# A four-layer network on one core: how attention blocks, the MLP's result and the edge layer's start leave PSUM

## The chip, the cores and the metric

The kernel runs on one core of one Trainium2 chip. The metric is the device time of one execution in microseconds (us); lower is better. Before the change it is 3922.71 us, the median of three runs from 3920.85 to 3927.91 us.

## The reference, cut to what matters

Four layers run one after the other on four images of 56 x 56 tokens with 128 channels, all in fp32. The change lies in layer 0 and at the start of layer 1.

```python
# layer 0: x = x + L0(group_norm(x))
xf = windowed_attention(shifted 7x7 windows of x) @ wo + bo      # 64 windows of 49 tokens
xf = xf + mha(layernorm(xf), wq, bq, wk, bk, wv, bv, wo, bo)     # 4 heads of 32, all 3136 tokens
h  = gelu(layernorm(xf) @ w1 + b1)                               # 128 -> 512
xf = xf + (h @ w2 + b2)                                          # 512 -> 128
# layer 1: x = x + L1(group_norm(x)), on rows of 56 nodes
edge = relu(x @ W1 [i] + x @ W2 [j] + be)                        # every pair i, j of a row
node = relu([x, edge.sum(over j)] @ Wn + bn)
```

Layers 2 (a Fourier layer with attention) and 3 (a convolution) follow. They take the second part of the span and are not touched.

## The kernel before, in words

**Layout.** Channels lie on the 128 partitions and tokens along the free dimension. An image is `xf`, 128 x 3136 fp32. A block is `NB` = 448 tokens, so an image has `NBLK` = 7 blocks. The four images go one after the other through `first_layers`: windowed attention, attention over all tokens (`fast_attention`), the MLP (`mlp`) and the edge layer (`edge_layer`). The image's input stays in `xw`, which the MLP adds back as the residual.

**Who sets the order.** In `fast_attention` and `mlp` TensorE's order is the order in which the program is written (`manual_schedule`); a scheduler places the instructions of the other engines. In the main loop of `edge_layer` the order of TensorE, ScalarE and VectorE is all as written. [...]

**Attention over all tokens.** For each block `j` of queries, 24 chunks of 128 keys and one of 64 are processed, with four heads each. TensorE writes scores into one of two PSUM tiles, `f_s0` with four banks and `f_s1` with three; ScalarE turns a whole tile into exponentials in a ring of 28 slots in SBUF (`f_ring`, line 641); TensorE multiplies these with the values into `f_po` (line 600); VectorE adds up 22 of the chunks (`f_acc`, line 594) for the denominators. At a block's end ScalarE copies `f_po` to `f_raw`, and `finish(j)` uses the next score tile: TensorE sums the exponentials over keys into its first bank (lines 607 and 610), VectorE takes the reciprocal straight out of that bank (line 612) and multiplies (line 613) into `oT`. The next scores that want this tile wait until the reciprocal has read it. `finish` is put off by some tiles (`late`, `flush`), so the next block's scores start ahead of it. After all seven blocks a loop projects each with `wo` into `f_pf`, in a pool slot that holds one bank, and VectorE adds that, with the bias, to `xf` (lines 663 and 664).

**MLP.** The tokens are taken in eight parts of 392. TensorE centres each part (`m_pc`, line 670), ScalarE squares it, TensorE averages (`n_pv`), ScalarE takes the root (line 682), and VectorE the reciprocal and the product (lines 683 and 868). Then for each part come four matmuls with GELU, and four that sum into `m_po`, of which there are two buffers. VectorE writes `xf` + `m_po` + `b2` (line 877), which frees the buffer. GpSimd adds `xw` and puts the result into image order in `x1` with three additions, since the windows are shifted by three and wrap around (lines 883 to 886). VectorE takes statistics of every seven rows (line 887).

**Start of the edge layer.** `group_norm_factors` aggregates the statistics and needs one square root on ScalarE (line 2338), after GELU was the last function there. Then VectorE normalizes all seven blocks into `e_xg` (line 192), and `project` makes `e_pa` and `e_pc` (lines 922 and 924) for the first two blocks. ScalarE copies them to `e_c` and `e_a` (lines 932 and 934). VectorE takes 9 of every 14 groups of pairs (`e_td`, line 967, straight from `e_pa` in PSUM), GpSimd and ScalarE the other 5 (`e_tp`, lines 969 and 971).

Of the kernel before, what the change touches and what calls it, by code (L numbers as in the profile page):

```python
# [11 lines left out]
F32 = mybir.dt.float32  # L12
AF = mybir.ActivationFunctionType
ALU = mybir.AluOpType
# [4 lines left out]
P = 128  # L19
# [20 lines left out]
def blk(j):  # L40
    return slice(j * NB, (j + 1) * NB)
# [149 lines left out]
def apply_norm(k, out, xt, mr):  # L191
    k.nc.vector.tensor_scalar(out, xt, mr[:, 0:1], mr[:, 1:2], ALU.subtract, ALU.mult)
# [367 lines left out]
def fast_attention(k, w, xw, xf, mr):  # L560

    nc, tc = k.nc, k.tc
    scale = 1.0 / math.sqrt(32.0)
    heads = [slice(32 * h, 32 * h + 32) for h in range(4)]
    half = (slice(0, 64), slice(64, 128))
    with ExitStack() as es:  # L570
        big = es.enter_context(tc.tile_pool(name="f_big", bufs=1))
        qT = big.tile([P, TOK], F32, name="f_qT")
        kT = big.tile([P, TOK], F32, name="f_kT")
        va = big.tile([P, 25, P], F32, name="f_va")
        fast_windows(k, w, xw, xf, mr, qT, kT, va)

        ring = es.enter_context(tc.tile_pool(name="f_ring", bufs=1)).tile([P, RING, NB], F32, name="f_ring")
        wk = es.enter_context(tc.tile_pool(name="f_wk", bufs=2))
        ps = es.enter_context(tc.tile_pool(name="f_ps", bufs=1, space=PSUM))
        oT = es.enter_context(tc.tile_pool(name="f_out", bufs=1)).tile([P, TOK], F32, name="f_oT")  # L580
        late = []
        n = 0

        def bank(turn):
            return ps.tile([P, (4, 3)[turn], 512], F32, tag="s%d" % turn, name="f_s%d" % turn)

        def slots(j, c):
            s = (96 * j + 4 * c) % RING
            return ring[:, s:s + 4, :]

        def sums(j, c, acc):

            if 0 < c < SUMMED:
                nc.vector.tensor_add(acc, slots(j, 0) if c == 1 else acc, slots(j, c))  # L594

        def values(j, c, po, p24):
            for h in range(4):
                o = half[h % 2] if c == 24 else slice(0, P)
                p = p24[o, h // 2, :] if c == 24 else slots(j, c)[:, h, :]
                nc.tensor.matmul(po[heads[h], :NB], va[o, c, heads[h]], p, start=(c == 0), stop=(c == 24))  # L600

        def finish(j, raw, acc, p24, pd):

            for c in range(SUMMED - 1, 24):
                p = acc if c < SUMMED else slots(j, c)
                for h in range(4):
                    nc.tensor.matmul(pd[heads[h], 0, :NB], k.ones[:, 0:32], p[:, h, :], start=(c < SUMMED), stop=False)
            for h in range(4):
                o = half[h % 2]
                nc.tensor.matmul(pd[heads[h], 0, :NB], k.ones[o, 0:32], p24[o, h // 2, :], start=False, stop=True)  # L610
            den = wk.tile([P, NB], F32, name="f_den")
            nc.vector.reciprocal(den, pd[:, 0, :NB])  # L612
            nc.vector.tensor_mul(oT[:, blk(j)], raw, den)

        def flush(all_=False):

            nonlocal n
            if n % 2 and not all_:
                return
            while late and (all_ or late[0][0] < n):  # L620
                _, f, *a = late.pop(0)
                if f is finish:
                    a.append(bank(n % 2))
                    n += 1
                f(*a)

        with tc.manual_schedule(engines={mybir.EngineType.PE}):
            for j in range(NBLK):
                po = ps.tile([P, 512], F32, tag="po", name="f_po")
                raw = wk.tile([P, NB], F32, name="f_raw")  # L630
                acc = wk.tile([P, 4, NB], F32, name="f_acc")
                t, done = 0, 0
                while t < 96:
                    turn, slot = n % 2, (96 * j + t) % RING
                    m = min((4, 3)[turn], RING - slot, 96 - t)
                    ss = bank(turn)
                    for i in range(m):
                        c, h = divmod(t + i, 4)
                        nc.tensor.matmul(ss[:, i, :NB], kT[heads[h], c * P:(c + 1) * P], qT[heads[h], blk(j)],  # L639
                                         start=True, stop=True)  # L640
                    nc.scalar.activation(ring[:, slot:slot + m, :], ss[:, :m, :NB], AF.Exp, scale=scale)  # L641
                    t += m
                    while 4 * (done + 1) <= t:
                        sums(j, done, acc)
                        late.append((n + 2, values, j, done, po, None))
                        done += 1
                    n += 1
                    flush()
                ss = bank(n % 2)
                for h in range(4):  # L650
                    nc.tensor.matmul(ss[half[h % 2], h // 2, :NB], kT[heads[h], 24 * P:TOK], qT[heads[h], blk(j)],
                                     start=True, stop=True)
                p24 = wk.tile([P, 2, NB], F32, name="f_p24")
                nc.scalar.activation(p24, ss[:, 0:2, :NB], AF.Exp, scale=scale)
                late.append((n + 2, values, j, 24, po, p24))
                late.append((n + 2, nc.scalar.copy, raw, po[:, :NB]))
                late.append((n + 3, finish, j, raw, acc, p24))
                n += 1
                flush()
            flush(True)  # L660
        for j in range(NBLK):
            pm = ps.tile([P, 512], F32, tag="po", name="f_pf")
            nc.tensor.matmul(pm[:, :NB], w.wo, oT[:, blk(j)], start=True, stop=True)
            nc.vector.scalar_tensor_tensor(xf[:, blk(j)], pm[:, :NB], w.fbvo, xf[:, blk(j)], ALU.add, ALU.add)


def centre(k, pool, centred, src, squares, j):
# [171 lines left out]
def mlp(k, w, xf, xw, x1, st):  # L839
# [4 lines left out]
    with ExitStack() as es:  # L844
# [25 lines left out]
        for wi, ts in enumerate(parts):  # L870
            hT = ahead
            if wi < 7:
                ahead = hidden(parts[wi + 1])
            po = psum.tile([P, 512], F32, tag="acc", name="m_po")
            for f in range(4):
                nc.tensor.matmul(po[:, :N], w.w2[:, f, :], hT[:, f, :], start=(f == 0), stop=(f == 3))
            nc.vector.scalar_tensor_tensor(xf[:, ts], po[:, :N], w.b2, xf[:, ts], ALU.add, ALU.add)
            a = xf[:, ts].rearrange("p (w i j) -> p w i j", w=8, i=7)
            x = xw[:, ts].rearrange("p (w i j) -> p w i j", w=8, i=7)
            for i0, i1 in (((0, 7),) if wi < 7 else ((0, 4), (4, 7))):  # L880
                r0 = (7 * wi + 3 + i0) % HH
                rows = x1[:, r0:r0 + i1 - i0, :]
                nc.gpsimd.tensor_add(  # L883
                    rows[:, :, 3:52].rearrange("p i (w j) -> p w i j", w=7), a[:, 0:7, i0:i1, :], x[:, 0:7, i0:i1, :])
                nc.gpsimd.tensor_add(rows[:, :, 52:56], a[:, 7, i0:i1, 0:4], x[:, 7, i0:i1, 0:4])
                nc.gpsimd.tensor_add(rows[:, :, 0:3], a[:, 7, i0:i1, 4:7], x[:, 7, i0:i1, 4:7])
                nc.vector.bn_stats(st[:, wi + (i0 > 0), :], rows.rearrange("p l n -> p (l n)"))

# [3 lines left out]
def edge_layer(k, w, x1, st):  # L894
# [9 lines left out]
    with ExitStack() as es:  # L904
# [6 lines left out]

        mr = group_norm_factors(k, wk, bank, st)
        xg = big.tile([P, TOK], F32, name="e_xg")
        for j in range(NBLK):
            apply_norm(k, xg[:, blk(j)], xf[:, blk(j)], mr)
        ready = {}

        def project(j):
            if j >= NBLK:
                return  # L920
            pa = psum.tile([P, 512], F32, tag="pa", name="e_pa")
            nc.tensor.matmul(pa[:, :NB], w.W1, xg[:, blk(j)], start=True, stop=True)
            pc = psum.tile([P, 512], F32, tag="mm", name="e_pc")
            nc.tensor.matmul(pc[:, :NB], w.W2, xg[:, blk(j)], start=True, stop=True)
            ready[j] = pa, pc

        def evacuate(j):
# [21 lines left out]
            nc.vector.scalar_tensor_tensor(xf[:, blk(j)], po[:, :NB], w.nbn, xf[:, blk(j)], ALU.max, ALU.add)  # L949

        with tc.manual_schedule(engines={mybir.EngineType.PE, mybir.EngineType.Activation, mybir.EngineType.DVE}):
            for j in range(2):
                project(j)
                evacuate(j)
            last = None
            for j in range(NBLK):
# [4 lines left out]
                for g, e in enumerate(EDGE_TURNS):  # L961
# [18 lines left out]
                        evacuate(j + 1)  # L980
                    if g == 7 and last:
                        finish(last[0], po)
                    if g == 9:
                        nc.vector.tensor_reduce(rest, c[:, :, 0:nd], AX.X, ALU.add)
                sums = wk.tile([P, 4, NB], F32, name="e_sums")
# [1480 lines left out]
```

## Time and profile before

| Image 0, us from the start of the span | what | TensorE clock granted | TensorE busy |
|---|---|---|---|
| 157 to 526 | attention over all tokens, seven blocks | 1.00 | 353.56 of 369 |
| 526 to 544 | last reciprocal, and the projections with `wo` | 0.67 | 10.72 of 18 |
| 544 to 574 | MLP: norm, and hidden layers of the first parts | 0.92 | 29.58 of 30 |
| 574 to 604 | MLP: the rest | 1.00 | 26.59 of 30 |
| 604 to 613 | factors of the group norm, start of the edge layer | 0.50 | 5.61 of 9 |
| 613 to 761 | edge layer | 1.00 | 141.33 of 148 |

Images 1, 2 and 3 repeat this about 710 us apart; layers 2 and 3 begin near 2890 us. In the lines of the profile, a time in square brackets is the time that the engine sat idle before the instruction, and behind the arrow stands what ended that idle time. A matmul in fp32 appears twice[...].

### The profile page before, as it was taken

How to read it: one execution, taken by the hardware profiler on the slowest of the kernel's cores; microseconds unless marked ns; L12 is line 12 of the kernel's file. 1: busy time of each engine (PE TensorE's matmuls, PEld its weight loads, DVE VectorE, ACT ScalarE, POOL GpSimd, SP SyncE). 2: the span in 40 equal slices, each digit the busy share in tenths (PEclk: the TensorE clock that was granted, in tenths of full speed). 3: DMA queues.
4: the chain of work that ended last, by engine and by line, in shares of the span. 5: the costliest groups of instructions: out<-in, count | busy, mean ns of one | idle time of the engine just before them, and what ended most of it. 6: DMA issues, size and time to landing. Idle time of an engine off the chain costs nothing. (4 is left out here: it accounts for less than half of the span.)

```text
span 3919.3 us, 79380 instructions
## 1 busy us (share of the span) xinstructions
PE 3543.1 (90%) x35416; PEld 1585.1 (40%) x35416; DVE 2883.2 (74%) x2667; ACT 2048.9 (52%) x2056; POOL 1201.0 (31%) x671
## 2 busy tenths in 40 slices
PE   6899988989998898999889999998977989999988
PEld 4322234542223455222245532224446433336554
DVE  6588867758887685888769568885975767775764
ACT  4577755557776444877555467773532011215332
POOL 0000006600000570000047100001860769984665
PEclk9999999999999999999999999998978999999988
DMA  2000000000000000000000000000022048842101
GB/s 95 1 1 1 1 1 19 19 1 1 1 1 1 18 13 7 1 1 1 1 17 3 18 1 1 1 1 0 3 77 96 2 91 168 174 95 83 58 9 50
DMA packets 73496, 111.12 MB, mean 28 GB/s; under 512 B 62140, under 2 KB 63932, under 8 KB 67900
## 3 DMA queue, kind: packets, MB, share of 16 engines
q1 hardware_dynamic: 14460, 93.13, 8.0%
q10 hardware_dynamic: 58688, 12.85, 2.0%
q8 instruction: 279, 4.57, 0.5%
q14 instruction: 69, 0.57, 0.0%
HBM read 79.46 MB, written 26.51 MB: 27 GB/s over the span
## 5 line engine op out<-in xcount | busy, mean ns | idle before, releaser
L641 ACT ACTIVATE f_ring<-f_s 128x1792 f32<-128x1792 f32 (+3 forms) x796 | 1098.2, 1430 | 318.2 <-PE f_s L639 315.9
L594 DVE TENSOR_TENSOR f_acc<-f_acc,f_ring 128x1792 f32<-128x1792 f32 x560 | 1134.1, 2025 | 82.0 <-ACT f_ring L641 28.2
L639 PE MATMUL f_s<-f_qT,f_kT 32*128 32x448 f32 x5376 | 742.1, 574 | 57.7 <-ACT f_ring L641 26.7
L883 POOL TENSOR_TENSOR x<-xf,xw 128x343 f32<-128x343 f32 (+2 forms) x36 | 30.0, 832 | 2125.9 <-issue 2053.6
L600 PE MATMUL f_po<-f_ring,f_va 128*32 128x448 f32 x5376 | 592.0, 548 | 0.0
L967 DVE TENSOR_TENSOR e_td<-e_pa,e_c 128x1792 f32<-128x1792 f32 x252 | 491.4, 2017 | 8.0 <-ACT e_a L934 8.0
L969 POOL TENSOR_TENSOR e_tp<-e_a,e_c 128x1792 f32<-128x1792 f32 x140 | 451.7, 3260 | 143.8 <-PE e_acc L974 104.5
L639 PEld LDWEIGHTS f_s<-f_qT,f_kT 32*128 32x128 f32 x5376 | 269.1, 184 | 538.9 <-ACT f_ring L641 369.1
L974 PE MATMUL e_acc<-e_td,t_shared 32*32 32x448 f32 x8064 | 321.9, 545 | 24.9 <-DVE e_td L967 14.2
L971 ACT ACTIVATE e_tp<-e_tp 128x1792 f32<-128x1792 f32 x140 | 235.1, 1697 | 185.9 <-POOL e_tp L969 185.9
L1568 DVE TENSOR_TENSOR u_ud<-u_px,u_d 112x1792 f32<-112x1792 f32 x144 | 240.1, 1708 | 95.1 <-PE u_po L1573 86.0
L600 PEld LDWEIGHTS f_po<-f_ring,f_va 128*32 128x32 f32 x5376 | 133.0, 109 | 400.8 <-issue 399.8
L974 PE MATMUL e_acc<-e_tp,t_shared 32*32 32x448 f32 x4480 | 220.4, 544 | 2.4 <-ACT e_tp L971 2.2
L1573 PE MATMUL u_po<-u_ud,AT 112*64 112x448 f32 x960 | 200.7, 548 | 23.7 <-DVE u_ud L1568 23.7
L1570 POOL TENSOR_TENSOR u_up<-xh,u_d 112x1792 f32<-112x1792 f32 x64 | 193.8, 3054 | 24.1 <-PE u_po L1573 12.4
L974 PEld LDWEIGHTS e_acc<-e_td,t_shared 32*32 32x32 f32 x8064 | 133.4, 103 | 149.6 <-DVE e_td L967 59.9
L594 DVE TENSOR_TENSOR f_acc<-f_ring 128x1792 f32<-128x1792 f32 x28 | 56.7, 2025 | 106.8 <-ACT f_ring L641 77.9
L1573 PE MATMUL u_po<-u_up,AT 112*64 112x448 f32 x576 | 125.1, 541 | 0.9 <-POOL u_up L1570 0.9
L1573 PEld LDWEIGHTS u_po<-u_ud,AT 112*64 112x64 f32 x960 | 64.8, 137 | 148.0 <-issue 86.7
L974 PEld LDWEIGHTS e_acc<-e_tp,t_shared 32*32 32x32 f32 x4480 | 94.4, 103 | 54.6 <-ACT e_tp L971 18.6
L856 ACT ACTIVATE m_hT<-m_ph,w_fb 128x392 f32<-128x392 f32 x128 | 72.7, 589 | 73.4 <-PE m_ph L855 67.9
L612 DVE RECIPROCAL f_den<-f_s 128x448 f32<-128x448 f32 x28 | 82.8, 2956 | 37.5 <-PE f_s L610 37.5
(460 smaller groups left out, 4738.5 us busy)
## 6 DMA issues: line engine op xcount, KB each, us to landing
u_d<-dd SPq DMA_DIRECT2D x48, 784.0 KB
xw<-in_x SPq DMA_DIRECT2D x4, 1568.0 KB
x2d<-x SPq DMA_DIRECT2D x4, 1568.0 KB
x_xs<-xad ACTq DMA_DIRECT2D x32, 196.0 KB
xm<-x_ev ACTq DMA_DIRECT2D x64, 98.0 KB
o_a<-xm SPq DMA_DIRECT2D x8, 784.0 KB
o_x<-x2d SPq DMA_DIRECT2D x4, 1568.0 KB
out<-o_o SPq DMA_DIRECT2D x12, 448.0 KB
```

Of the source, the lines that this page charges most:

```text
L594: nc.vector.tensor_add(acc, slots(j, 0) if c == 1 else acc, slots(j, c))
L600: nc.tensor.matmul(po[heads[h], :NB], va[o, c, heads[h]], p, start=(c == 0), stop=(c == 24))
L612: nc.vector.reciprocal(den, pd[:, 0, :NB])
L639: nc.tensor.matmul(ss[:, i, :NB], kT[heads[h], c * P:(c + 1) * P], qT[heads[h], blk(j)], start=True, stop=True)
L641: nc.scalar.activation(ring[:, slot:slot + m, :], ss[:, :m, :NB], AF.Exp, scale=scale)
L967: nc.vector.tensor_tensor(t, am, cm, ALU.max)
L969: nc.gpsimd.tensor_sub(t, bc(a.rearrange("p (l n) -> p l n", l=8), 1, 4), cm)
L971: nc.scalar.activation(tf, tf, AF.Relu)
L974: nc.tensor.matmul(acc[quarters[q], r, :NB], k.ident[o, o], t[o, q].rearrange("p l n -> p (l n)"), start=(g == 0), stop=(g == len(EDGE_TUR ...
L1568: nc.vector.tensor_mul(u, bc(px[:, :, :NB], 2, m), dm)
L1570: nc.gpsimd.tensor_mul(u, bc(x, 2, m), dm)
L1573: nc.tensor.matmul(po[64 * b2:64 * b2 + 64, :NB], st.AT[:, 8 * i + h0 + q, 2 * bp + b2, :], u[:, b2, q, :], start=(left == 16), stop=(left ...
```

## The change

It has three places, all in layers 0 and 1.

- Attention: in `finish(j)` TensorE also projects the previous block, into the second bank of the same score tile, and one ScalarE copy takes both the denominators and that projected block out of PSUM. The reciprocal and the addition to `xf` then read SBUF. Only the last block is still projected after the loop. The purpose is to free the score tile earlier and to spread the projections over the blocks.
- MLP: VectorE first adds `xw` and `b2` to `xf`, which needs no matmul; then the three additions into `x1` [...] run on VectorE in place of GpSimd. At the end of the MLP ScalarE takes a square root of something that isn't used, so that the table of the root is in place ahead of the group norm.
- Edge layer: VectorE normalizes only the first two blocks ahead; ScalarE normalizes block `j + 2` during block `j`. `e_pc` is made before `e_pa`.

```diff
         def finish(j, raw, acc, p24, pd):
 ...
-            den = wk.tile([P, NB], F32, name="f_den")
-            nc.vector.reciprocal(den, pd[:, 0, :NB])
-            nc.vector.tensor_mul(oT[:, blk(j)], raw, den)
+            m = 1 + (j > 0)
+            if j:
+                nc.tensor.matmul(pd[:, 1, :NB], w.wo, oT[:, blk(j - 1)], start=True, stop=True)
+            den = wk.tile([P, 2, NB], F32, name="f_den")
+            nc.scalar.copy(den[:, :m], pd[:, :m, :NB])
+            nc.vector.reciprocal(den[:, 0], den[:, 0])
+            nc.vector.tensor_mul(oT[:, blk(j)], raw, den[:, 0])
+            if j:
+                output(j - 1, den[:, 1])
+
+        def output(j, pm):
+            nc.vector.scalar_tensor_tensor(xf[:, blk(j)], pm, w.fbvo, xf[:, blk(j)], ALU.add, ALU.add)
 ...
-        for j in range(NBLK):
-            pm = ps.tile([P, 512], F32, tag="po", name="f_pf")
-            nc.tensor.matmul(pm[:, :NB], w.wo, oT[:, blk(j)], start=True, stop=True)
-            nc.vector.scalar_tensor_tensor(xf[:, blk(j)], pm[:, :NB], w.fbvo, xf[:, blk(j)], ALU.add, ALU.add)
+        pm = ps.tile([P, 512], F32, tag="po", name="f_pf")
+        nc.tensor.matmul(pm[:, :NB], w.wo, oT[:, blk(NBLK - 1)], start=True, stop=True)
+        output(NBLK - 1, pm[:, :NB])
 ...
-            nc.vector.scalar_tensor_tensor(xf[:, ts], po[:, :N], w.b2, xf[:, ts], ALU.add, ALU.add)
+            nc.vector.scalar_tensor_tensor(xf[:, ts], xf[:, ts], w.b2, xw[:, ts], ALU.add, ALU.add)
             a = xf[:, ts].rearrange("p (w i j) -> p w i j", w=8, i=7)
-            x = xw[:, ts].rearrange("p (w i j) -> p w i j", w=8, i=7)
+            x = po[:, :N].rearrange("p (w i j) -> p w i j", w=8, i=7)
 ...
-                nc.gpsimd.tensor_add(      # and two more
+                nc.vector.tensor_add(      # and two more
 ...
+        nc.scalar.activation(wk.tile([P, 1], F32, name="m_root"), hT[:, 3, 0:1], AF.Sqrt, bias=k.eps, scale=0.0)
 ...
-        for j in range(NBLK):
-            apply_norm(k, xg[:, blk(j)], xf[:, blk(j)], mr)
+        shift = wk.tile([P, 1], F32, name="e_shift", bufs=1)
+        nc.vector.tensor_scalar(shift, mr[:, 0:1], mr[:, 1:2], -1.0, ALU.mult, ALU.mult)
 ...
+        def normed(j):
+            if j < 2:
+                apply_norm(k, xg[:, blk(j)], xf[:, blk(j)], mr)
+            elif j < NBLK:
+                nc.scalar.activation(xg[:, blk(j)], xf[:, blk(j)], AF.Identity, bias=shift, scale=mr[:, 1:2])
 ...
-            pa = psum.tile([P, 512], F32, tag="pa", name="e_pa")
-            nc.tensor.matmul(pa[:, :NB], w.W1, xg[:, blk(j)], start=True, stop=True)
             pc = psum.tile([P, 512], F32, tag="mm", name="e_pc")
             nc.tensor.matmul(pc[:, :NB], w.W2, xg[:, blk(j)], start=True, stop=True)
+            pa = psum.tile([P, 512], F32, tag="pa", name="e_pa")
+            nc.tensor.matmul(pa[:, :NB], w.W1, xg[:, blk(j)], start=True, stop=True)
 ...
+                    if g == 8:
+                        normed(j + 2)
```

More of the change, by code (lines that the diff above doesn't have):

```diff
@@ L882, in mlp @@
                 rows = x1[:, r0:r0 + i1 - i0, :]
-                nc.gpsimd.tensor_add(
+                nc.vector.tensor_add(
                     rows[:, :, 3:52].rearrange("p i (w j) -> p w i j", w=7), a[:, 0:7, i0:i1, :], x[:, 0:7, i0:i1, :])
-                nc.gpsimd.tensor_add(rows[:, :, 52:56], a[:, 7, i0:i1, 0:4], x[:, 7, i0:i1, 0:4])
-                nc.gpsimd.tensor_add(rows[:, :, 0:3], a[:, 7, i0:i1, 4:7], x[:, 7, i0:i1, 4:7])
+                nc.vector.tensor_add(rows[:, :, 52:56], a[:, 7, i0:i1, 0:4], x[:, 7, i0:i1, 0:4])
+                nc.vector.tensor_add(rows[:, :, 0:3], a[:, 7, i0:i1, 4:7], x[:, 7, i0:i1, 4:7])
                 nc.vector.bn_stats(st[:, wi + (i0 > 0), :], rows.rearrange("p l n -> p (l n)"))
+        nc.scalar.activation(wk.tile([P, 1], F32, name="m_root"), hT[:, 3, 0:1], AF.Sqrt, bias=k.eps, scale=0.0)
 EDGE_TURNS = "ddpddpdpddpddp"
@@ L920, in project @@
                 return
+            pc = psum.tile([P, 512], F32, tag="mm", name="e_pc")
+            nc.tensor.matmul(pc[:, :NB], w.W2, xg[:, blk(j)], start=True, stop=True)
             pa = psum.tile([P, 512], F32, tag="pa", name="e_pa")
             nc.tensor.matmul(pa[:, :NB], w.W1, xg[:, blk(j)], start=True, stop=True)
-            pc = psum.tile([P, 512], F32, tag="mm", name="e_pc")
-            nc.tensor.matmul(pc[:, :NB], w.W2, xg[:, blk(j)], start=True, stop=True)
             ready[j] = pa, pc
@@ L951, in edge_layer @@
         with tc.manual_schedule(engines={mybir.EngineType.PE, mybir.EngineType.Activation, mybir.EngineType.DVE}):
+            for j in range(2):
+                normed(j)
             for j in range(2):
```

## The prediction, made before the changed kernel ran

> **What bounds the kernel now.** I read the busy shares first (TensorE 90%, VectorE 74%, ScalarE 52%), then the chain of waits for layers 0 and 1, then the order of time at each place that the change touches. An average share doesn't price a change; the chain says which engine a stage waits for. At the end of a block in attention (image 3) it reads: start, us, what.
>
> ```profile
> 2334.09 2.46 PE f_s L607 x24
> 2336.55 0.93 PE f_s L610 x8
> 2337.48 0.02 issue
> 2337.50 2.97 DVE f_den L612
> 2340.47 0.04 issue
> 2340.51 1.77 PE f_s L639 x12
> ```
>
> The reader is to see that the reciprocal stands on the path: the next scores wait until it has left their PSUM tile. But the wait is short, because other matmuls lie between. The group of the reciprocals' tile says so: "PE f_s L639: 11.0, 24", which is 0.46 us for each. Behind the seventh block, in image 0, TensorE and VectorE take turns on one PSUM bank:
>
> ```profile
> 525.95 1.02 PE L663 MATMUL f_pf<-f_oT,t_first 128*128 128x448 f32 x2
> 526.09 2.96 DVE L612 RECIPROCAL f_den<-f_s 128x448 f32<-128x448 f32 x1 [3.56 <-PE f_s L610]
> 528.97 0.58 DVE L664 SCALAR_TENSOR_TENSOR xf<-f_pf,w_fbvo,xf 128x448 f32<-128x448 f32 x1
> 529.47 0.62 DVE L613 TENSOR_TENSOR f_oT<-f_raw,f_den 128x448 f32<-128x448 f32 x1
> ...
> 541.38 1.86 PE L663 MATMUL f_pf<-f_oT,t_first 128*128 128x448 f32 x2 [0.78 <-DVE xf L664]
> 543.28 0.68 DVE L664 SCALAR_TENSOR_TENSOR xf<-f_pf,w_fbvo,xf 128x448 f32<-128x448 f32 x1 [1.96 <-PE f_pf L663]
> 544.01 1.68 PE L670 MATMUL m_pc<-xf,c_centre 128*128 128x392 f32 x2 [0.78 <-DVE xf L664]
> ```
>
> The turns last 2.64 us each, since the matmul has slowed from 1.02 to 1.86 us. The MLP then waits for VectorE's eight reciprocals, until the addition that frees `m_po` (chain, image 3):
>
> ```profile
> 2697.52 4.97 DVE n_r L683 x2
> 2702.50 0.89 DVE m_y L868 x2
> 2703.39 0.55 DVE xf L877
> 2703.94 0.04 issue
> 2703.98 2.90 PE m_po L876 x8
> ```
>
> From there to the end of the MLP TensorE is the bound, and behind it the group norm is one chain (image 0):
>
> ```profile
> 606.17 1.28 ACT L2338 ACT_TABLE_LOAD   x1 [10.23 <-PE e_mm L2337]
> 607.47 0.26 ACT L2338 ACTIVATE gf_t<-e_mm,c_eps 128x1 f32<-128x1 f32 x1
> ...
> 612.46 0.52 ACT L934 COPY e_a<-e_pa 128x448 f32<-128x448 f32 x1
> 613.01 2.02 DVE L967 TENSOR_TENSOR e_td<-e_pa,e_c 128x1792 f32<-128x1792 f32 x1 [2.00 <-ACT e_a L934]
> ```
>
> [...] `e_td` waits for the copy `e_a`, whose result it doesn't read: it starts at 613.01, when that ends at 612.98.
>
> **Attention, inside the loop.** Each `finish` but the first adds one projection, about 0.88 us of TensorE's path (525.07 to 525.95 is the pitch of a matmul group in that place). ScalarE's copy has 128x896 elements; the exponential of that shape, from PSUM, takes 0.92 us (line 654), and that of one block 0.54 (line 625). ScalarE is idle for 3.7 to 5.6 us there before its next exponential, so it costs nothing itself. It ends before TensorE is back at the tile, so the stall goes. By the pitches at the six finishes in image 0, the tile is reached 0.35 us earlier in the first, 0.44 later in three (0.88 less the stall of some 0.42) and 0.58 later in two: -0.35 + 3 x 0.44 + 2 x 0.58 = **+2.1 us an image**.
>
> VectorE's reciprocal now waits for projection and copy, 1.8 us more, and an addition to `xf` (0.5 to 0.6 us) is queued ahead of the product: 2.4 us later for the additions `f_acc` behind it, for which the next `finish` waits. In image 0 the last addition ended 2.95, 2.75, 3.66 and 4.8 us ahead of that use in the blocks after finishes 1 to 4. The first finish has no projection, and behind the fifth VectorE idles for 2.19 us. So I cost it at nothing.
>
> **Attention, the tail.** From the end of line 610 to the first `m_pc` it took 18.06 us in image 0 (525.95 to 544.01), 14.42, 18.63 and 18.15 in the others (in image 1 the clock stayed up). After: projection and copy 1.9, reciprocal 2.9, addition 0.5, product 0.6, the last projection 1.86 (TensorE has been idle for 5 us, so I take the slow value; 1.02 is the other end), addition 0.7, with hand-overs 8.65. Gains 9.4 + 5.8 + 10.0 + 9.5 = **-34.7 us**.
>
> **MLP, front.** In the built program four of the new additions (xf + b2 + xw) stand in VectorE's queue ahead of the first reciprocal. Each needs `m_pc` of its part to have read `xf`, so the reciprocals now wait for the fourth `m_pc`. In image 0 that ended at 550.73; with an addition of 0.54 the first reciprocal starts 7.3 us behind the first `m_pc`, and it was 5.83. By the same reading the delays are 1.5, 2.7 (there 4.61 before), 0.7 to 1.5 and 1.5. All queued behind it is on the path until `m_po` is freed, now by three additions out of PSUM instead of one. Such a small addition is not in the trace; between 0.16 (128x1, line 2331) and 0.25 (GpSimd's own), so about 0.9 against 0.63. Sum 6.8 + 4 x 0.3 = **+8.0 us**.
>
> **MLP, end.** From `m_po` to the aggregate it took 600.62 to 603.57, 2.95 us, in a relay of VectorE and GpSimd. On VectorE alone: two larger additions 0.4 and 0.35, four small ones 0.7, statistics 0.73, about 2.1: **-3.4 us** for four images. In the parts before, VectorE's 2.1 us a part hide beside TensorE's 5.27. The freed GpSimd was waiting there anyway: nothing.
>
> **Table.** 606.17 to 607.47 goes; the new load follows the last GELU, where ScalarE idles for 10.23 us: **-5.2 us**.
>
> **Edge.** A shift of 0.2 is added ahead of the norms. With `e_pc` first, `e_c` is copied while `e_pa` is made, and only the copy `e_a` follows: `e_td` starts 4.92 us after the root's reciprocal instead of 5.25: **-1.3 us**. The five norms taken from VectorE lay in a wait (idle 2.00 before `e_td`), so they give nothing; on ScalarE, 0.68 each like line 935, they fall into a gap of 1.5 us in the first block and of 5.25 in later ones.
>
> Sum: 2.1 x 4 - 34.7 + 8.0 - 3.4 - 5.2 - 1.3 = -28.2, so 3894 us. Layers 2 and 3 keep their order and just start earlier.
>
> **Rivals.** *A, as worked out: 3894 us.* *B, more:* the clock survives the short tail. Then the last projection saves 0.85 and the fourth `m_pc` comes 2.2 us sooner: 3 us an image, 3882; if the projections in the loop cost nothing either, 3874. Image 1's tail, warm throughout, speaks for it; TensorE falling to half speed after idling for 3 to 5 us before line 922 in all images speaks against. *C, slower:* VectorE is late in attention and each of the 24 later finishes costs its 2.4 us, 57.6 in place of 8.4: 3943. The sixth block speaks for it, where TensorE waited 1.53 us for `f_acc`; the margins of 2.75 us and more speak against. Half of it gives 3919, no change.
>
> **How the numbers follow.** A 0.72, B 0.18, half of C 0.06, C 0.04. Faster by over 0.2% (below 3914.9) is A and B, 0.90; no change 0.06; slower 0.04. The range, 3878 to 3908, holds A with 0.2 us either way for each small addition and half a microsecond for each finish, and most of B.
>
> **What would show it.** The tail is 8 to 9 us, with one `f_pf` an image. TensorE's wait for `f_den` is gone and none for `f_acc` is new outside the last block. The first reciprocal of the MLP starts about 7 us behind the first `m_pc`, with four additions ahead of it. The table load follows GELU. I am wrong if the seven blocks of image 0 take over 3 us more than 369, or if the edge layer's blocks, 20.5 us apart, change.

## The result, and the profile after

The kernel after takes 3904.4 us (median of four runs, 3900.0 to 3907.5) against 3925.3 us for the kernel before on the same chip: ratio 0.9945, 95% interval 0.9928 to 0.9963, so 14 to 28 us less. The forecast was 3894 us, and its range from 3878 to 3908 holds the result. Of the ten microseconds between, 2.6 are the kernel before itself, which was at 3922.7 when the forecast was made. The others don't lie where the change is: those stages together gained more than was forecast. They lie in stages that the change doesn't touch. Inside the change one step cost 5.5 us where 1.2 were forecast, and larger gains elsewhere cover it.

**Attention.** The first view is TensorE's waits in the seven blocks of image 0 (who waited, for whom: us in total, times, longest). Before, with the row for `f_den`:

```profile
PE f_s L639 <- DVE f_den L612: 2.7, 6, 1.2
PE f_s L607 <- DVE f_acc L594: 1.5, 1, 1.5
```

After:

```profile
PE f_s L649 <- ACT f_ring L651: 6.0, 9, 2.4
PE f_s L608 <- ACT f_ring L651: 2.6, 5, 1.1
PE f_s L608 <- DVE f_acc L594: 1.5, 1, 1.5
```

The row for `f_den` is gone. The only wait for `f_acc` is the 1.5 us that were there before (6.4 us in the four images, and 6.1 before), so VectorE's later start costs next to nothing. The tail of the same image, in order of time (start, us, engine, what, idle time before it and what ended it):

```profile
533.37 1.02 PE L614 MATMUL f_s<-f_oT,t_first 128*128 128x448 f32 x2
534.43 0.91 ACT L616 COPY f_den<-f_s 128x896 f32<-128x896 f32 x1 [5.26 <-PE f_s L614]
535.37 2.95 DVE L617 RECIPROCAL f_den<-f_den 128x448 f32<-128x448 f32 x1 [5.42 <-ACT f_den L616]
538.24 0.59 DVE L623 SCALAR_TENSOR_TENSOR xf<-f_den,w_fbvo,xf 128x448 f32<-128x448 f32 x1
538.74 0.62 DVE L618 TENSOR_TENSOR f_oT<-f_raw,f_den 128x448 f32<-128x448 f32 x1
539.50 1.83 PE L672 MATMUL f_pf<-f_oT,t_first 128*128 128x448 f32 x2 [5.11 <-DVE f_oT L618]
541.38 0.69 DVE L623 SCALAR_TENSOR_TENSOR xf<-f_pf,w_fbvo,xf 128x448 f32<-128x448 f32 x1 [2.02 <-PE f_pf L672]
542.21 2.95 PE L679 MATMUL m_pc<-xf,c_centre 128*128 128x392 f32 x4 [0.87 <-DVE xf L623]
```

One `f_pf` is left. From the end of the denominators' matmuls to the first `m_pc` it takes 8.76 us, in all four images. The last projection is slow (1.83 us, where the one in the last finish took 1.02), at a granted clock of 0.50, so the clock did not survive the tail.

**MLP.** The same view of its start, and of the third `m_po`. Before:

```profile
549.84 2.60 DVE L683 RECIPROCAL n_r<-n_r 128x392 f32<-128x392 f32 x1 [5.88 <-ACT n_r L682]
...
573.99 2.90 PE L876 MATMUL m_po<-m_hT,t_first 128*128 128x392 f32 x8 [0.40 <-DVE xf L877]
```

After:

```profile
549.46 0.63 DVE L886 SCALAR_TENSOR_TENSOR xf<-xf,t_first,xw 128x392 f32<-128x392 f32 x1 [1.02 <-PE m_pc L679]
550.00 5.06 DVE L692 RECIPROCAL n_r<-n_r 128x392 f32<-128x392 f32 x2
...
574.29 4.26 PE L885 MATMUL m_po<-m_hT,t_first 128*128 128x392 f32 x8 [2.02 <-DVE x L895]
```

L886 at 549.46 is the fourth residual addition; the first reciprocal comes after it, 7.79 us behind the first `m_pc` (5.83 before). At its far end the delay meets TensorE: it waits 2.02 us for `m_po` (0.40 before), and then the eight matmuls take 4.26 us instead of 2.90. The windows of that stretch say why (us, busy time of TensorE, its weight loads, VectorE, ScalarE and GpSimd, then the granted clock, DMA share and GB/s):

```profile
574.30:576.00 1.70, 1.70 (x5) 1.09 (x6) 1.70 (x6) 0.00 (x0) 0.00 (x0) 0.89 0.00 0
576.00:578.00 2.00, 2.00 (x4) 1.04 (x4) 1.29 (x3) 0.00 (x0) 0.00 (x0) 0.50 0.02 4
```

The granted clock falls from 1.00 to 0.50 behind that wait.

**Table and edge layer**, in order of time:

```profile
597.93 1.28 ACT L898 ACT_TABLE_LOAD   x1
...
606.45 0.26 ACT L2359 ACTIVATE gf_t<-e_mm,c_eps 128x1 f32<-128x1 f32 x1 [6.93 <-PE e_mm L2358]
...
611.59 5.89 DVE L986 TENSOR_TENSOR e_td<-e_pa,e_c 128x1792 f32<-128x1792 f32 x3 [3.59 <-ACT e_a L951]
```

The load now lies under the last matmuls of the MLP, and the root starts at once.

Both kernels were profiled a second time (e9, e10 below). Sums over the four images, in us, with the places that separate them:

| stage | before | again | after | again | forecast | change of the means |
|---|---|---|---|---|---|---|
| first scores to the last denominators | 1502.2 | 1502.0 | 1509.0 | 1508.1 | +8.4 | +6.5 |
| to the first `m_pc` (the tail) | 69.0 | 74.3 | 35.0 | 35.0 | -34.7 | -36.6 |
| to the MLP's first reciprocal | 22.1 | 23.3 | 29.1 | 29.0 | +6.8 | +6.4 |
| to the end of the last `m_po` | 203.0 | 203.0 | 208.5 | 208.5 | +1.2 | +5.5 |
| to the aggregate | 11.9 | 11.9 | 6.7 | 6.8 | -3.4 | -5.2 |
| to the root's reciprocal | 16.2 | 16.6 | 10.3 | 10.4 | -5.2 | -6.0 |
| to the first `e_td` | 21.0 | 21.0 | 19.4 | 19.4 | -1.3 | -1.6 |
| edge layer from there | 598.0 | 599.3 | 598.0 | 597.9 | 0 | -0.7 |
| all ahead of the scores | 448.7 | 446.6 | 453.7 | 449.3 | 0 | +3.9 |
| layers 2 and 3 | 1027.3 | 1028.9 | 1035.8 | 1031.7 | 0 | +5.7 |

By these means the stages that the change touches gained 31.7 us, more than the forecast 28.2, and 9.6 were given back in the last two rows, in places whose instructions are the same. That leaves 22.1, beside 20.9 by the medians. So the total lies in the range partly because errors of both signs cancel.

### The profile page after: what moved, and what is told of

Read it like the earlier page. It is cut to its first block, busy times and chain, and to the rows that moved or that the text cites. A ratio compares the mean times of both kernels' runs of the same rounds, so it can differ in the third digit from the quotient of the medians.

```text
span 3905.7 us, 79417 instructions
## 1 busy us (share of the span) xinstructions
PE 3553.4 (91%) x35416; PEld 1604.1 (41%) x35416; DVE 2891.3 (74%) x2759; ACT 2086.9 (53%) x2108; POOL 1156.6 (30%) x563
## 5 line engine op out<-in xcount | busy, mean ns | idle before, releaser
L993 PE MATMUL e_acc<-e_td,t_shared 32*32 32x448 f32 x8064 | 322.2, 545 | 20.9 <-DVE e_td L986 10.0
L1594 PE MATMUL u_po<-u_ud,AT 112*64 112x448 f32 x960 | 200.7, 548 | 23.3 <-DVE u_ud L1589 23.3
L617 DVE RECIPROCAL f_den<-f_den 128x448 f32<-128x448 f32 x28 | 82.7, 2953 | 77.5 <-ACT f_den L616 77.5
L993 PEld LDWEIGHTS e_acc<-e_tp,t_shared 32*32 32x32 f32 x4480 | 94.4, 103 | 55.3 <-ACT e_tp L990 19.4
L1456 POOL TENSOR_TENSOR q_u<-iS,q_g 128x1792 f32<-128x1792 f32 x32 | 102.8, 3236 | 23.9 <-PE q_acc L1471 23.9
```

The source lines that it names most:

```text
L993: nc.tensor.matmul(acc[quarters[q], r, :NB], k.ident[o, o], t[o, q].rearrange("p l n -> p (l n)"), start=(g == 0), stop=(g == len(EDGE_TUR ...
L1594: nc.tensor.matmul(po[64 * b2:64 * b2 + 64, :NB], st.AT[:, 8 * i + h0 + q, 2 * bp + b2, :], u[:, b2, q, :], start=(left == 16), stop=(left ...
```

## The experiments

Each was compared with the kernel before by medians on the same chip (e9 to e12 are profiles alone). Differences in us are the ratio less one, times before's median.

**e1: the attention part alone.** The `finish` and tail of the diff, nothing else.

> The kernel before with the attention part of the change alone. Theory (the gain is the attention tail, and the MLP part gives some of it back): from the end of the last denominators' matmuls to the first m_pc 8.8 us in each image instead of 18.0, 14.4, 18.6 and 18.1, so -34; the seven blocks cost about +1.7 us an image, so +7; MLP, table and edge layer as before, with the first reciprocal of the MLP 4.6 to 5.9 us behind the first m_pc. About -27 us, that is 6 us more than the whole change brought. Rival (the MLP part is no loss, and the missing part of the attention's gain lies in the loop): no more than -14 us, since the whole change brought -20.9 and the table, the MLP's end and the edge layer gave some 12 of these.

Ratio 0.9943 (0.9929 to 0.9957), -22.4 us. The stages came as the theory has them: tail 8.76 us in every image, first reciprocal of the MLP 5.79 us behind the first `m_pc`, in sum -28 us from the first scores to the end of the edge layer, against the first profile of before. But layers 2 and 3 took 1040.4 us, 13 more than in the first profile of before. So the part alone brings as much as the whole change, the rival's -14 is out, and what is missing from the theory's -27 lies in this last stage.

**e2: the MLP part alone**, without the early root.

```diff
-            nc.vector.scalar_tensor_tensor(xf[:, ts], po[:, :N], w.b2, xf[:, ts], ALU.add, ALU.add)
+            nc.vector.scalar_tensor_tensor(xf[:, ts], xf[:, ts], w.b2, xw[:, ts], ALU.add, ALU.add)
...
-                nc.gpsimd.tensor_add(      # and two more, from xw
+                nc.vector.tensor_add(      # and two more, from po
```

> The kernel before with the MLP part alone: the residual added ahead, the three additions out of PSUM on VectorE; no early root table. Theory (the four residual additions in VectorE's queue hold the reciprocals until the fourth m_pc is through, and the longer wait of TensorE ahead of the third m_po costs it its clock): first reciprocal 6 to 8 us behind the first m_pc instead of 4.6 to 5.8 (+7 in four images), from there to the last m_po +5.5, from there to the aggregate -5.2: slower by about 7 us. Rival (as forecast, only the delay and three additions in place of one): +8.0 - 3.4 = +4.6 us. Second rival (the freed GpSimd and the shorter end win): faster by 5 us.

Ratio 1.0018 (1.0009 to 1.0027), +7.1 us: slower than before, and the second rival is out. But that the time agrees with the theory is luck. The first reciprocal came 6.3 to 7.2 us behind the first `m_pc` (+4.8 in sum), but to the last `m_po` it lost 2.2 and not 5.5 us, since only image 1 lost the clock, and the MLP's end gained 5.1. So in its own stages the part lost only 1 to 2 us in this trace (1.9 against the first profile of before, 1.2 against the mean of both); layers 2 and 3, which it doesn't touch, took 1043.7 us. The first rival's +4.6 lies within the interval and is not told apart. The waits ahead of the third `m_po` were 1.86, 2.02, 1.23 and 1.10 us, and the eight matmuls took 2.87, 4.56, 2.87 and 2.87.

**e3: the early table and the edge layer's part alone.**

> The kernel before with the early root table and the edge layer's part alone. Theory: the table load goes from the path (-1.3 to -1.6 us an image, -5.5), the edge layer starts 0.4 us earlier (-1.6): about -7 us in all, and its blocks stay 20.5 us apart. Rival (the added norms on ScalarE disturb the blocks): no gain, blocks further apart than 20.5 us. Rival (the load is hidden, or moved to another place on the path): -1.6 us alone.

Ratio 0.9979 (0.9969 to 0.9988), -8.2 us, as the theory says. The trace has -5.1 for the table and -1.6 for the start, and the blocks stay 20.53 us apart, so neither rival holds.

The three parts sum to -23.5 us; the whole gave -21.6 by its ratio. In the stages they are not independent: from the first `m_pc` to the aggregate the MLP takes 237.6 us in the four images before (mean of the two profiles), 238.8 in e2 and 244.3 after. Behind the short tail three images of four lost the clock (4.26 to 4.57 us for the eight matmuls, 2.87 in the fourth), and in e2 one (4.56).

**e4: the residual off VectorE's queue.**

```diff
-            nc.vector.scalar_tensor_tensor(xf[:, ts], xf[:, ts], w.b2, xw[:, ts], ALU.add, ALU.add)
+            nc.gpsimd.tensor_scalar(xw[:, ts], xw[:, ts], w.b2, None, ALU.add)
+            nc.gpsimd.tensor_add(xf[:, ts], xf[:, ts], xw[:, ts])
```

> The kernel after, but the addition of residual and bias (xf + b2 + xw) is made by GpSimd in two steps (xw + b2, then xf + that), so that it is not in VectorE's queue. Theory (the order in VectorE's queue is what the MLP part loses): the first reciprocal starts no later than 4.6 to 5.9 us behind the first m_pc, TensorE's wait ahead of the third m_po is 0.4 us or less longer than in the kernel before, its clock stays up; 9 to 12 us faster than the kernel after, about 3893 us, -31 against the kernel before. Rival (the delay is the order of m_pc itself, or the three additions out of PSUM that free m_po): within 3 us of the kernel after. Rival (two GpSimd operations a part come late for the additions into x1): slower than the kernel after, with VectorE waiting for GpSimd at lines 893 to 896.

Ratio 0.9914 (0.9901 to 0.9928), -33.8 us, 3894.9 us: 12 us better than the kernel after by the ratios, 7.5 in the MLP's stages (236.8 us against 244.3). The first reciprocal is back at 5.79 us, and no image loses its clock (2.87 us for the eight matmuls). But the wait was 1.12 to 1.48 us, not 0.4 more than before, so about 0.9 us an image remains. In order of time:

```profile
546.04 1.01 POOL L887 TENSOR_TENSOR xf<-xf,xw 128x392 f32<-128x392 f32 x1 [0.40 <-ACT n_r L691]
...
547.00 1.79 DVE L877 TENSOR_TENSOR m_y<-m_y,n_r 128x392 f32<-128x392 f32 x2
547.26 1.11 POOL L887 TENSOR_TENSOR xf<-xf,xw 128x392 f32<-128x392 f32 x1 [0.21 <-POOL xf L887]
```

The pair of products at L877 takes 1.79 us where GpSimd adds beside it, and 0.97 in the later pairs. No run shows what the 0.82 us between them come from.

**e7: the same cure on VectorE**, to tell its order from its load.

```diff
-            nc.vector.scalar_tensor_tensor(xf[:, ts], xf[:, ts], w.b2, xw[:, ts], ALU.add, ALU.add)
+            nc.vector.scalar_tensor_tensor(xw[:, ts], po[:, :N], w.b2, xw[:, ts], ALU.add, ALU.add)
...
-            x = po[:, :N].rearrange("p (w i j) -> p w i j", w=8, i=7)
+            x = xw[:, ts].rearrange("p (w i j) -> p w i j", w=8, i=7)
```

> The kernel after with another first step in the MLP: xw = m_po + b2 + xw on VectorE, one addition that needs the matmul and frees m_po, and then the three additions xf + xw into x1 on VectorE out of SBUF. As many VectorE instructions as in the kernel after, only the first of them can't be ahead of the reciprocals. Theory (order in VectorE's queue, not its load): first reciprocal 5.8 us behind the first m_pc, wait ahead of the third m_po 0.5 us as before and not 2.0, its matmuls at full clock (2.9 us for the group and not 4.3 to 4.6), from the last m_po to the aggregate 2.1 to 2.3 us (one addition more than after): 10 to 11 us faster than the kernel after, about 3894 us. Rival (load on VectorE): no faster than the kernel after.

Ratio 0.9920 (0.9906 to 0.9933), -31.4 us. As many VectorE instructions as after, and yet 5.79 us to the first reciprocal and 50.74 to the last `m_po`, as in the kernel before:

```profile
569.50 2.90 PE L885 MATMUL m_po<-m_hT,t_first 128*128 128x392 f32 x8 [0.19 <-DVE xw L886]
```

From the last `m_po` to the aggregate it takes 2.38 us (1.69 after), a little over the forecast. The MLP's stages take 235.7 us, 8.6 less than after and 1.9 less than before. Neither run changes the order in the queue alone: e7 also frees `m_po` by one addition again, and e4, which frees it by three, takes load off VectorE. But each keeps what the other takes away, so neither the load nor the three additions is the loss. What both undo is the order, and in both no image lost the clock.

**e5: ScalarE's copy alone.** The projections stay behind the loop.

```diff
-            nc.vector.reciprocal(den, pd[:, 0, :NB])
+            nc.scalar.copy(den, pd[:, 0, :NB])
+            nc.vector.reciprocal(den, den)
```

> The kernel before with one edit: ScalarE copies the denominators (one block, no projection) out of the score tile and the reciprocal reads the copy; the projections stay behind the loop. Theory (the copy buys the end of TensorE's short wait for the tile, 0.46 us in each of 24 finishes, and no more): the seven blocks of an image take about 2.5 us less, the tail is 0.6 to 0.7 us longer for the copy: -10 + 2.5 = about -8 us, TensorE's wait for f_den gone. Rival (the copy itself delays the tail and the additions for the denominators as much as it frees the tile): within 2 us of before. Second rival (the copy is the main part of the change's gain): -15 us or more.

Ratio 1.0011 (1.0003 to 1.0020), +4.3 us. The theory's sum fails, though its stages hold: the blocks sum to 1490.9 us, -11.2, and the wait for `f_den` is gone; the tails sum to 77.8, 3.5 more than in the second profile of before. Layers 2 and 3 took 1033.9 us. The copy is not the main part of the gain.

**e6: the projections in the loop, without the copy.** The reciprocal reads `pd[:, 0]` and the addition to `xf` reads `pd[:, 1]`, both in PSUM.

> The attention part alone, but without ScalarE's copy: the projection of the previous block lies in the second bank of the score tile, the reciprocal and the addition to xf read PSUM directly. Theory: the tile is now held through reciprocal and addition (and the product, if it stands between), 0.17 to 0.79 us of wait per finish on top of 0.88 us of projection, so the seven blocks take 3.5 to 7 us an image more than before instead of 1.2 (attention part with the copy); the tail is 0.9 us shorter than the 8.8 with the copy, for want of it. In sum 5 to 20 us slower than the attention part with the copy, and still 3 to 17 us faster than before. Rival (spreading the projections is all that matters, the copy is idle work): as fast as the attention part with the copy, -22 us, or better by the copy's 0.9 us in each tail.

Ratio 0.9969 (0.9956 to 0.9981), -12.2 us: between, as the theory says, and 10 us short of e1. The tail is shorter (7.1 to 7.7 us), but the blocks take 6.4 us an image more than before. A finish in image 0:

```profile
264.18 2.96 DVE L616 RECIPROCAL f_den<-f_s 128x448 f32<-128x448 f32 x1 [5.21 <-PE f_s L614]
...
267.05 0.58 DVE L622 SCALAR_TENSOR_TENSOR xf<-f_s,w_fbvo,xf 128x448 f32<-128x448 f32 x1
...
267.78 2.29 PE L648 MATMUL f_s<-f_qT,f_kT 32*128 32x448 f32 x14 [1.80 <-DVE xf L622]
```

TensorE waits for the addition, which now holds the tile, and its granted clock falls to 0.50 from 268.9 to 272.3 us. That is what the copy is for: with the projection in the loop it keeps two VectorE instructions, here of 2.96 and 0.58 us, from holding the tile.

**e8: e7, and the last finish's addition off VectorE.**

```diff
-            if j:
-                output(j - 1, den[:, 1])
+            if j == NBLK - 1:
+                nc.gpsimd.tensor_scalar(den[:, 1], den[:, 1], w.fbvo, None, ALU.add)
+                nc.gpsimd.tensor_add(xf[:, blk(j - 1)], xf[:, blk(j - 1)], den[:, 1])
+            elif j:
+                output(j - 1, den[:, 1])
```

> The kernel of e7_one_addition, and in the last finish of each image GpSimd adds the projected block to xf in two steps in the shadow of the reciprocal, so that VectorE goes from the reciprocal straight to the product. Theory (the addition stands on the path of the tail, between reciprocal and product, for 0.5 us): the tail is 8.2 to 8.3 us instead of 8.76, 2 us less in all than e7. Rival (GpSimd's work beside VectorE slows the reciprocal by as much, or comes late for the first m_pc): a tail of 8.76 us or more.

Ratio 0.9924 (0.9911 to 0.9938), -29.9 us, no different from e7. The tail is 8.38 us, 0.38 less and not 0.5: GpSimd's two steps of 1.41 and 1.12 us do fit under the reciprocal, but 1.5 us in all is below what these comparisons resolve. e4, e7 and e8 all beat the kernel before. Against the kernel after, the intervals of e7 and e8 overlap with its own, so that they beat it rests on the MLP's stages, which are 8.6 us shorter in both.

**e9 and e10: the two kernels once more.**

> The kernel before, unchanged, profiled a second time. What it is for: in the stages that the change touches the traces differ by -27 us (before to after), but the medians by -21. Theory (the rest lies outside the change and is chance of the single execution): layers 2 and 3, which took 1027.3 us in the first profile, take some other time between 1025 and 1044 us here; the tail of image 1, 14.35 us in the first profile, is 18 us like the other images; the MLP (5.8, 50.7 and 3.0 us) and the edge layer (149.0) repeat within 0.1 us. Rival (the change makes the later layers slower): 1027 +- 1.5 us again.

> The kernel after, unchanged, profiled a second time. Theory: layers 2 and 3, 1035.8 us in the first profile, take some other time between 1025 and 1044 us; the tail is 8.76 us again in all images; the wait ahead of the third m_po is 1.2 or 2.0 us, and its eight matmuls take 2.9 us where it is 1.2 and over 4.2 where it is 2.0. Rival (the change makes the later layers slower): 1036 +- 1.5 us again.

The MLP and the edge layer repeat within 0.1 us in nearly all images (one edge layer of before took 152.32 us instead of 150.94). Image 1's tail in before was 18.11 us this time: the 14.35 that the forecast used (as 14.42) was that one execution's, and so were the 4.61 us to its first reciprocal (5.83 this time). After repeats its tails to 0.01 us, and the waits of 2.02, 2.02, 2.02 and 1.17 us with 4.34, 4.52, 4.57 and 2.87 us for the matmuls. Layers 2 and 3 took 1028.9 us in before, 1.6 more than in the first profile, and 1031.7 in after, 4.1 less. So they vary within one kernel, but after stayed above before. The rival's 1036 us is out in after; before repeats within little more than the 1.5 us that its rival allows.

**e11 and e12: e5 and e1 once more**, for that reason.

> The kernel of e5_copy_only, profiled a second time: its trace has 8 us less in attention and its tail than the second profile of before, yet its median was 4 us above. Theory (the gain in attention is real and is lost by chance of clock in layers 2 and 3): the seven blocks sum to 1491 +- 2 us and the tails to 78 +- 1.5 us again, layers 2 and 3 take more than 1034 us here. Rival (the first profile was not typical in attention): blocks of 1497 us or more.

> The kernel of e1_att_only, profiled a second time: layers 2 and 3 took 1040.4 us in its first profile. Theory (chance of the single execution): attention, tail, MLP and edge layer repeat within 2 us in sum (2415 us), layers 2 and 3 differ from 1040.4 by more than 3 us. Rival (an earlier end of layer 1 makes the later layers slower by itself): 1040 +- 2 us again.

The attention of e5 repeats (1489.2 us, tails 78.7), and layers 2 and 3 took 1044.2 us, 10 more than in its first profile. e1 repeats too, and there they took 1041.1, which is the number that the rival forecast. But its reason, an earlier end of layer 1, doesn't hold in the other runs: layer 1 ended at 2891.7 and 2890.7 us in the two profiles of e5, as in the first of before (2892.0), and e6 ended it at 2883.3 and then took 1028.9. A window of 250 us that starts 700 us behind the end of layer 1 shows the difference, first in the kernel before, then in e11 (the columns as above):

```profile
3592.00:3842.00 250.00, 228.63 (x1552) 150.93 (x1544) 159.77 (x280) 98.86 (x132) 155.97 (x94) 0.90 0.09 33
```

```profile
3590.70:3840.70 250.00, 230.71 (x1472) 152.46 (x1469) 153.75 (x263) 89.94 (x122) 143.95 (x88) 0.82 0.08 27
```

Granted clock 0.90 against 0.82, and fewer instructions done in the same time. It is 0.90 in both profiles of before, in e3 and in e6; 0.87 and 0.89 in after; 0.82 and 0.85 in e1; 0.87 and 0.82 in e5; 0.82 in e2 and e4, 0.85 in e7 and e8. So a part of what attention gains is given back in layer 3, at a lower granted clock, in a stretch whose instructions are the same.

By their time in layers 2 and 3 the fourteen profiles fall into two groups. It was 1027 to 1032 us in five: both of before, e3, e6 and the second of after. It was 1034 to 1044 us in the other nine: the first of after, both of e1 and of e5, and e2, e4, e7 and e8. So one kernel, after, stands in both. What puts an execution into one of them is not shown. Nor is it shown why eight of the nine profiles with ScalarE's copy in attention lie on the slow side, and four of the five without it on the fast side.

## Why the prediction was right, and where it was not

- **Tail, -34.7: right**, 35.0 us left of a forecast of 34.6. Its credit of 5.8 us for image 1 was too small by 3.6, as the clock in image 1's tail stayed at 1.00 in that execution of before (each projection 1.02 us, 14.35 us in all), while the second took 18.11 us there. That the last projection would be slow was an estimate, 1.86 us; it took 1.83.
- **Blocks, +8.4: right, 2 us too high.** The forecast was five projections of 0.88 us in each image, 17.6 in all, less 9.2 for TensorE's waits for `f_den`. The copy alone (e5) takes 11.2 us from the loops, so these waits were priced 2 us too low; by subtraction from +6.5 the projections cost 17.7.
- **VectorE's delay of 2.4 us at nothing: right.** No new wait for `f_acc`; C didn't happen.
- **MLP front, the queue: right in its mechanism, and in its sum partly by luck**, +6.4 against +6.8. By image (first profiles) the delays were 2.0, 3.0, 1.7 and 0.5 us against 1.5, 2.7, 0.7 to 1.5 and 1.5, and image 1's is counted against the odd 4.61. The forecast took the fourth `m_pc` where before has it; after, it ended 7.2 us behind the first in image 0 (6.7 before), where the clock came up after 6.1 us, and 5.7 in image 3, where it came up after 3.1. e4 and e7 show the cause by taking it away.
- **Freeing `m_po`, 4 x 0.3 = 1.2 us: too small, the step that failed.** It measured 5.5. The forecast took the third `m_po` as a wait that moves by as much as its releaser does, with everything behind it at full speed; what the longer wait does to TensorE's clock it put at nothing. In three images of four TensorE waited 2.02 us instead of 0.40 to 0.55 and its clock then fell to 0.50: 1.81 us each, 1.4 to 1.7 of it in the eight matmuls. The fourth image waited 1.20, kept its clock and lost 0.12.
- **MLP end, -3.4: too small**, -5.2. The small additions take 0.15 to 0.18 us, but the next starts 0.06 to 0.09 behind, so the last four took 0.4 us and not 0.7; the two larger took 0.5 and not 0.75.
- **Table, -5.2, and edge, -1.3: right**, -6.0 and -1.6. The two matmuls `e_mm` got shorter as well (in image 0 0.35 and 0.38 us, from 0.56 and 0.59), which the forecast doesn't have.
- **Layers 2 and 3 "keep their order and just start earlier": the order holds, the time doesn't.** They took 5.7 us longer in the mean of the profiles of after. With 3.9 us ahead of the scores this is more than what the forecast missed. The two profiles of after differ by 4.1 us themselves (1035.8 and 1031.7), so the order of the instructions alone doesn't give this stage its time.
- **B**, that the clock survives the tail, is refuted by the 1.83 us of the last projection, at a granted clock of 0.50, in all four images.
- **Two readings are inexact, without bearing on the sum.** Line 625 is a copy of one block and not an exponential, and ahead of line 922 TensorE idled 2.44 us, after 3.53 and 0.83 us ahead of the two `e_mm`.

## What to carry to other kernels

An operation that needs no late input is not free to go early: look at what it needs (here `m_pc` reading `xf`), and at what stands behind it in its engine's queue (here the reciprocals, 7.79 us behind the first `m_pc` instead of 5.83). Written so that it needs the late input after all (e7), the same work no longer delayed them (5.79). And price a wait of TensorE not by its length alone but also by the matmuls behind it, which may run at half the clock (here 1.4 to 1.7 us more in eight of them), and take a stage's time from more than one execution before crediting a change with an odd one out, or charging it with one.

## What the hardware showed beyond the forecast

- A short wait was followed by a stretch at half the clock. In image 0 of after TensorE waited for the third `m_po` from 572.27 to 574.29 us; the granted clock was 0.50 from 575.62 to 579.03, and 1.00 right before and right behind (columns as in the windows above):

```profile
572.21:575.62 3.41, 1.39 (x5) 0.87 (x5) 3.41 (x11) 0.61 (x2) 0.00 (x0) 1.00 0.00 0
575.62:579.03 3.41, 3.41 (x7) 1.69 (x6) 2.11 (x6) 0.00 (x0) 0.00 (x0) 0.50 0.01 2
579.03:582.44 3.41, 3.41 (x12) 2.02 (x11) 1.26 (x5) 2.35 (x4) 0.00 (x0) 1.00 0.47 132
```

- The waits of 2.02 us ahead of the third `m_po` were followed by it in seven cases of seven (three images in each profile of after, one in e2); the eight matmuls then took 4.26 to 4.57 us instead of 2.87 to 2.90. Behind waits of 1.10 to 1.48 us (the fourth image of after, two of e2, and e4) they took 2.87. In between both occurred: no fall behind 1.86 us (e2), a fall to 0.50 behind 1.80 us ahead of other matmuls (e6). So the length of a wait alone didn't tell, and what else counts isn't shown.
- VectorE's small additions out of PSUM in after took 0.15 to 0.18 us each, and the next addition started 0.06 to 0.09 us behind the start of one.
- A later layer ran at another granted clock, 0.82 to 0.90 over 250 us, though none of its instructions had changed, and one kernel, after, showed 0.87 in one execution and 0.89 in another (e5: 0.87 and 0.82).
